# A two-layer decoder with routed experts: phases of the last groups' latents, a block table in three pieces, and later slots for the empty rows

## The chip, the core and the metric

The kernel runs on one core of a Trainium2 chip. A core has engines that work side by side, each taking its own instructions strictly in order: PE multiplies matrices, DVE (vector), ACT (scalar) and POOL (general) work on elements, and SP does little but issue DMA transfers. They wait for each other by semaphores. Matmuls write to PSUM, which holds eight banks of 128 x 512 floats here; the other engines read the banks and so empty them. The metric is device time in microseconds (us) of a whole execution.

## The reference

It is a decoder of two layers over 32 batches of 128 tokens, 128 wide, with a context of 128 tokens by 96 per batch. Each of six blocks is added to x after a normalization. Cut to what matters:

```python
x = x + self_attention(ln(x))          # 16 heads of 8, rotated
x = x + cross_attention(ln(x), ctx)    # 16 heads of 8
x = x + gated_experts(ln(x))           # 8 routed (top 2), 2 shared, width 64
x = x + causal_attention(ln(x))        # 16 heads of 8, rotated
x = x + latents(ctx, ln(x), mask)      # the block that the change moves
x = x + experts(ln(x))                 # 8 experts, top 2, width 512, relu

def latents(ctx, lat, mask):           # 2 heads of 64
    lat, c = layernorm(lat), layernorm(ctx)
    q = lat @ Wq.T
    k, v = split(concat([c @ Wkv.T, lat @ Wlkv.T]))
    q, k = rmsnorm(q) * 64**-0.5, rmsnorm(k)
    return softmax(where(mask, q @ k.T, -max)) @ v @ Wo.T + bo

def experts(x):
    w, i = top_k(softmax(x @ router_w + router_b), 2);  w = w / sum(w)
    y[t, e] = relu(x[t] @ w1[e] + b1[e]) @ w2[e] + b2[e]
    return sum of w * y over the two chosen experts of each token
```

So each token of the latents attends to 256 keys, its batch's 128 latents and 128 context tokens, and each token of the last block goes to two of eight experts.

## The kernel before

**The plan.** The 32 batches are in 8 groups of 4; x stays on chip. The order on every engine is written out by hand. The three attentions of 16 heads give the beat: each is worked off in slots, two per batch, 64 per stage, 192 in all (`attention`). Everything else is laid beside them with `at(slot, phase, function)`. A loop walks through the slots and issues, in each, these phases in this order: "open", "pre", the slot's attention matmuls with their maxima and exps, "inner", the matmuls with the values of an earlier slot, "turn", "turned", "mid", "post". After slot 196 or so no attention is left, and a slot is only what was laid into it. Phases are not barriers: they fix the order in which each engine, SP and POOL's DMA issues among them, gets its instructions.

**Latents** (`latent_attention`). Group g starts at a slot d (L1244: two slots after its causal attention is done): d = 187 for group 5, 195 for group 6, 203 for group 7. In `plan_group`, statistics come at d, the norm's scales on POOL (L1082) at d + 1, the norm on ACT at d + 2 and d + 3, a transpose (L1111), q, k and v of the four batches (L1121) at d + 4 and d + 5, then sums of squares (L997), a pow on POOL (L1139) and the unit heads. Batch i of the group follows with t = d + 8 + 2i in `plan_batch`:

- `fetch` (t - 2, "mid"): SP loads the batch's context keys and values, `lkv<-kv` (L1181); three buffers.
- `turn` (t, "mid"): two transposes of q and k into one bank, emptied by ACT (L1186, L1188, L1189).
- `score` (t + 1, "mid"): per head a mask matmul and a score matmul (L1195, L1200), a maximum on DVE (L1206) and an exp on ACT (L1207).
- `turn_e` (t + 2, "mid"): four transposes of the exps into one bank, copied by DVE into leT (L1216).
- `weigh` (t + 3, "mid"): four matmuls with the values (L1226), then a reciprocal and a product on DVE into lon (L1230, L1232).

`leave` (d + 18, "mid") transposes the group's result, `project` (d + 19, "post") multiplies it by Wo (L1168) and adds it to x. All of these take PSUM banks from one pool, `ps_m`, whose three banks are handed out in turn: `turn`, `turn_e`, `weigh`, `leave`, `project` and each q, k, v take one, `score` takes two, and each waits until the bank of three takings before has been read.

**Router and slots.** From d + 19 on `plan_route` (L1588) chooses two experts per token and scatters the tokens' rows (128 numbers, a target, a gate) with indirect DMAs on POOL (L1729) into the `slots` of the experts in memory. There are three sets of slots, for groups 0 to 3, 4 and 5, and 6 and 7 (parts 0, 1, 2). Rows that no token takes must hold an empty row, whose target lies outside the result; `preset` (L2053) writes them from `nowhere` before any token comes, four transfers per part on SP, 2210 KB each for part 0, 1170 KB for the others. `once` lays preset n into slot 4 + 4n, "mid" (L2075).

**Experts** (`expert_blocks`). `table` (L1826) works out on DVE, on one partition, which expert and which 128 slots belong to each block of the part; the last operation writes the numbers that other engines read into registers. Then, for pairs of blocks: `fetch` on SP (`bx<-slots`, L1868), `weights` on ACT and DVE (a copy out of all experts' weights, L1871), `turn` (L1887, L1889), `hidden` (L1897; relu on ACT L1903 and DVE L1905), `result` (L1914; gates L1921, L1923), `leave` on POOL (an indirect DMA to y, L1928). `plan_part` (L1977) begins the parts at slots 209, 229 and 241, with 20, 12 and 12 pairs, one a slot from two slots later on; the table comes four slots ahead, four fetches are issued at once in the first slot, and each later slot issues one pair more. All experts' weights are loaded on SP in slots 205 on ("open", L1966, L1967).

**Gated experts** of the first layer lie beside the second attention. Each group writes its gates to memory and loads them back spread over the partitions, `g<-spread` (L921), two transfers on SP with a hold of x (L364) issued behind them; POOL and DVE multiply by them (L941), and PE uses the products (L950).

Of the kernel before, what the change touches and what calls it, by code (L numbers as in the profile page):

```python
# [11 lines left out]
F32 = mybir.dt.float32  # L12
# [16 lines left out]
E = 8  # L29
# [84 lines left out]
def decoder(ctx: ExitStack, tc: tile.TileContext, a: dict, out: bass.AP):  # L114
# [132 lines left out]
    def wide(t, shape, axis):  # L247
        return t.unsqueeze(axis).to_broadcast(shape)
# [809 lines left out]
    def latent_attention(lazy, kv, row, bias, masked, plan_route):  # L1058
# [12 lines left out]
        def plan_group(at, g, d):  # L1071
# [98 lines left out]
                nc.vector.tensor_tensor(xf, ps, xf, ALU.add)  # L1170

            at(d + 18, "mid", leave)
            at(d + 19, "post", project)
            plan_route(at, g, d + 19)

        def plan_batch(at, m, g, i, t):
# [57 lines left out]
                )  # L1234

            at(t - 2, "mid", fetch)
            at(t, "mid", turn)
            at(t + 1, "mid", score)
            at(t + 2, "mid", turn_e)
            at(t + 3, "mid", weigh)  # L1240

        def beside(at, done):
            for g in range(G):
# [575 lines left out]
    def expert_blocks(f, total, lazy):  # L1819

        room, nb, top_slot = ROOM[f], NB[f], SLOTS[f] - BLOCK
        y = tc.dram_tile([2 * room, D], F32, name=f"y{f}")
        state = {}
        where = []

        def table():  # L1826

            def row(shape, tag, dtype=F32):
                return lazy["blocks"].tile([1] + shape, dtype, tag="tb_" + tag, name="tb_" + tag, bufs=2 if tag == "where" else 1)

            count, blocks, end, skip = row([E], "count"), row([E], "blocks"), row([E], "end"), row([E], "skip")
            nc.vector.tensor_tensor(count, total[:1], e_base[f][:1], ALU.subtract)
            more = row([E, room // BLOCK], "more")
            nc.vector.tensor_tensor(
                more, wide(count, [1, E, room // BLOCK], 2), wide(starts[:1, : room // BLOCK], [1, E, room // BLOCK], 1), ALU.is_gt
            )
            nc.vector.tensor_reduce(blocks, more, AX.X, ALU.add)
            upto = row([E, E], "upto")
            nc.vector.tensor_tensor(upto, wide(blocks, [1, E, E], 1), until[:1], ALU.mult)
            nc.vector.tensor_reduce(end, upto, AX.X, ALU.add)  # L1840
            nc.vector.tensor_scalar(skip, blocks, -float(BLOCK), float(room), ALU.mult, ALU.add)
            past, t = row([nb, E], "past"), row([nb, E], "past_t")
            first = row([3, nb], "first")
            nc.vector.tensor_tensor(past, wide(end, [1, nb, E], 1), wide(numbers[:1, :nb], [1, nb, E], 2), ALU.is_le)
            nc.vector.tensor_reduce(first[:, 0, :], past, AX.X, ALU.add)
            nc.vector.tensor_tensor(t, past, wide(skip, [1, nb, E], 1), ALU.mult)
            nc.vector.tensor_reduce(first[:, 1, :], t, AX.X, ALU.add)
            nc.vector.tensor_tensor(first[:, 1, :], first[:, 1, :], starts[:1, :nb], ALU.add)
            nc.vector.tensor_scalar(first[:, 2, :], first[:, 0, :], float(E - 1), 512.0, ALU.min, ALU.mult)
            nc.vector.tensor_scalar(first[:, 0, :], first[:, 0, :], float(E - 1), float(W1), ALU.min, ALU.mult)  # L1850
            where.append(row([3, nb], "where", I32))
            nc.vector.tensor_copy(where[0], first)
# [95 lines left out]
            nc.gpsimd.tensor_tensor(one, one, two, ALU.add)  # L1948
            nc.vector.tensor_tensor(X[g], X[g], one, ALU.add)

        return table, fetch, weights, turn, hidden, result, leave, gather, finish

    def experts(halves, lazy, heads, late):

        def beside(at, done):
            def swap():
                heads.close()
                lazy["blocks"] = late.enter_context(tc.tile_pool(name="blocks", bufs=3, reuse_waits="tile"))

            def keep(e):  # L1960
                def fn():
                    rows = a["w_f"][e * P : (e + 1) * P]
                    if e == 0:
                        for tag, n in (("w1", W1), ("w2", 512)):
                            lazy[tag] = lazy["blocks"].tile([P, E * n], F32, tag=tag, name="all_" + tag, bufs=1)
                    nc.sync.dma_start(lazy["w1"][:, e * W1 : (e + 1) * W1], rows[:, :W1])  # L1966
                    nc.sync.dma_start(lazy["w2"][:, e * 512 : (e + 1) * 512], rows[:, W1:])  # L1967
                return fn

            at(done(2, G - 1) + 2, "open", swap)  # L1970
            for e in range(E):
                at(done(2, G - 1) + 2 + e, "open", keep(e))
            begins = [done(2, 3) + 40]
            begins.append(max(begins[0] + (NB[0] + 1) // 2, done(2, 5) + 40))
            begins.append(max(begins[1] + (NB[1] + 1) // 2, done(2, 7) + 33))

            def plan_part(f):  # L1977
                table, fetch, weights, turn, hidden, result, leave, gather, finish = halves[f]
                t = begins[f]
                pairs = (NB[f] + 1) // 2  # L1980
                at(t - 4, "mid", table)
                for i in range(4):
                    at(t, "post", lambda i=i: fetch(i))
                for i in range(2):
                    at(t + i, "post", lambda i=i: weights(i))
                at(t + 1, "post", lambda: turn(0))
                for i in range(pairs):
                    s = t + 2 + i
                    if i + 1 < pairs:
                        at(s, "pre", lambda i=i: turn(i + 1))  # L1990
                    at(s, "inner", lambda i=i: hidden(i))
                    at(s + 1, "post", lambda i=i: result(i))
                    at(s + 2, "mid", lambda i=i: leave(i))
                    if i + 4 < pairs:
                        at(s, "post", lambda i=i: fetch(i + 4))
                    if i + 2 < pairs:
                        at(s, "post", lambda i=i: weights(i + 2))
                if f + 1 < len(PARTS):
                    for n, g in enumerate(PARTS[f]):
                        at(begins[f + 1] + 6 + 2 * n, "post", lambda g=g: gather(g))  # L2000
                        at(begins[f + 1] + 8 + 2 * n, "post", lambda g=g: finish(g))
                        at(begins[f + 1] + 10 + 2 * n, "post", lambda g=g: store(g))

            for f in range(len(PARTS)):
                plan_part(f)
        return beside
# [46 lines left out]
    def preset(n):  # L2053

        chunks = SLOTS[n // 4] // (2 * P)
        part = slots[n // 4].rearrange("(c p r) w -> p c (r w)", p=P, r=2)[:, n % 4 * chunks // 4 : (n % 4 + 1) * chunks // 4]
        nc.sync.dma_start(
            part, nowhere.rearrange("p r w -> p (r w)").unsqueeze(1).to_broadcast([P, chunks // 4, 2 * ROW])
        )

    def once(at, done):
# [10 lines left out]
        at(107, "mid", lambda: folded_bias(w_o1, b_v1, b_o1, bias1))  # L2072
        at(108, "mid", lambda: folded_bias(w_xo1, b_vl, b_xo1, bias_l))
        for n in range(4 * len(PARTS)):
            at(4 + 4 * n, "mid", lambda n=n: preset(n))  # L2075
        guard = []
        at(138, "mid", lambda: guard.append(cross_guard(word)))
        at(140, "mid", lambda: guard[0]())
# [1 line left out]
    lazy, late = {}, ExitStack()  # L2080
# [123 lines left out]
```

## Time and profile before

| what | value |
|---|---|
| device time, median of 3 runs | 1142.7 us (1142.59 to 1147.51) |
| the profiled execution | 1184.79 us, its span 1183.1 us |
| mean granted clock of PE | 0.943 of full speed |
| PE matmul, busy | 1067.5 us (90%) in 12495 instructions |
| DVE, busy | 823.1 us (70%) in 2424 |
| POOL, busy | 645.3 us (55%) in 918 |
| ACT, busy | 615.8 us (52%) in 1440 |
| chain of work that ended last, by engine | PE 52%, DVE 19%, POOL 10%, ACT 7%, issue 6%, DMA 4% |
| moved by DMA | 71.24 MB, of these 37.02 MB written to memory |

The shares are means over stages that differ. Cut at the landmarks of the plan, PE is busy 168.52 of the first 190 us (start and first attention), 635.66 of the 671 up to 861 (second and third attention), 54.91 of the 67 up to 928 (no attention left, no expert matmul yet), 70.25 of the 78 up to 1006 (experts with the last latents beside them), 80.83 of the 99 up to 1105, and 57.33 of the last 78. The granted clock of these stretches is 0.95, 0.98, 0.70, 0.93, 0.88 and 0.90.

How to read the lines shown further on. An instruction in a timeline has its start and its length in us, the engine, the line of the code and the operation, then what it writes and reads; brackets hold the idle time of the engine just before it and what ended it. SPq is SP issuing a DMA: the start is that of the issue, not of the transfer. In the chain of waits each line is one step, start and length first. In a table by stretch the numbers behind an engine are busy us and, in brackets, a count of instructions.

### The profile page before, as it was taken

The page shows a single profiled execution, that of the slowest core. Times are in us where ns is not written, and L with a number is a line of the kernel's source. Part 1 is how long each engine was busy: PE and PEld are TensorE (multiplying, and loading weights), DVE is VectorE, ACT ScalarE, POOL GpSimd, SP SyncE. Part 2 cuts the span into 40 slices and gives each one's busy share as a digit, 9 for nine tenths or more (in the row PEclk, how much of TensorE's full clock was granted, in tenths as well). Part 3 has the DMA queues.
Part 4 walks back from the last instruction along what each step waited for, and adds up shares of the span by engine and source line. Part 5 has one row for each costly group of instructions (what it writes and reads, how often), then busy time and mean ns, then how long its engine had stood idle before and what let it go on. Part 6 is the DMA issues. An engine that isn't in the chain of part 4 may idle for free.

```text
span 1183.1 us, 32419 instructions
## 1 busy us (share of the span) xinstructions
PE 1067.5 (90%) x12495; PEld 829.2 (70%) x12495; DVE 823.1 (70%) x2424; ACT 615.8 (52%) x1440; POOL 645.3 (55%) x918
## 2 busy tenths in 40 slices
PE   6999999999999999999998999989988888788893
PEld 3666667677767776677667677767766778678893
DVE  4678878878778666867787788778666565454652
ACT  2356555676655555554555666744633543333551
POOL 4576656434442544235647675746837245555653
PEclk9999989999999999999999999989976899888997
DMA  8753331000121011110110000001115222123432
GB/s 204 220 154 101 101 100 61 29 29 29 38 47 46 7 41 37 38 26 14 38 46 7 11 15 15 16 11 35 31 37 157 69 56 58 38 66 86 107 109 77
DMA packets 77858, 71.24 MB, mean 60 GB/s; under 512 B 14554, under 2 KB 66829, under 8 KB 77696
## 3 DMA queue, kind: packets, MB, share of 16 engines
q1 hardware_dynamic: 72640, 60.08, 18.7%
q0 software_dynamic: 4768, 8.47, 2.1%
q8 instruction: 102, 1.67, 0.6%
q10 hardware_dynamic: 288, 0.52, 0.1%
q14 instruction: 60, 0.49, 0.1%
HBM read 33.39 MB, written 37.02 MB: 60 GB/s over the span
## 4 chain that ended last, share of the span: by engine, by line
PE 52%; DVE 19%; POOL 10%; ACT 7%; issue 6%; DMA 4%; SPq 0%; another core or an unknown queue 0%; DVEq 0%; POOLq 0%; ACTq 0%
PE bank L633 11%; PE bank L1897 5%; PE bank L661 5%; PE bank L1914 5%; DVE msc L636 5%; PE bank L950 3%; DMA g<-spread 3%; POOL h L941 2%; ACT e L644 2%; PE bank L1121 2%; PE bank L511 1%; PE bank L932 1%; DVE qa L540 1%; PE bank L1200 1%; PE bank L1226 1%
## 5 line engine op out<-in xcount | busy, mean ns | idle before, releaser
L644 ACT ACTIVATE e<-bank 128x512 f32<-128x512 f32 x384 | 207.6, 593 | 178.5 <-PE bank L633 174.2
L636 DVE TENSOR_REDUCE msc<-bank 128x4 f32<-128x512 f32 x384 | 245.2, 680 | 70.1 <-PE bank L633 67.1
L633 PE MATMUL bank<-kb,qz 32*128 32x256 f32 x1536 | 243.8, 410 | 12.3 <-DVE msc L636 10.5
L633 PE MATMUL bank<-qa,kb 32*128 32x128 f32 x3072 | 235.9, 289 | 4.5 <-ACT e L644 4.5
L633 PEld LDWEIGHTS bank<-qa,kb 32*128 32x128 f32 x3072 | 196.6, 191 | 9.7 <-ACT e L644 8.8
L633 PEld LDWEIGHTS bank<-kb,qz 32*128 32x128 f32 x1536 | 146.8, 190 | 65.1 <-DVE msc L636 33.2
L1928 POOL DMA_INDIRECT y<-bo,bx x85 | 85.3, 1004 | 81.5 <-ACT bo L1921 44.0
L647 POOL TENSOR_SCALAR_AFFINE_SELECT e<-e 128x512 f32<-128x512 f32 x128 | 79.2, 642 | 69.5 <-ACT e L644 69.2
L661 PE MATMUL bank<-e,vt 128*32 128x128 f32 x3072 | 109.3, 284 | 0.5 <-POOL e L647 0.5
L1897 PE MATMUL bank<-bxT,w 128*128 128x128 f32 x680 | 92.1, 287 | 9.9 <-issue 9.4
L1897 PEld LDWEIGHTS bank<-bxT,w 128*128 128x128 f32 x680 | 85.9, 202 | 12.5 <-issue 12.0
L1914 PE MATMUL bank<-all_w,bh 128*128 x680 | 91.3, 289 | 3.6 <-issue 3.5
L661 PEld LDWEIGHTS bank<-e,vt 128*32 128x32 f32 x3072 | 81.5, 113 | 15.7 <-POOL e L647 1.5
L1914 PEld LDWEIGHTS bank<-all_w,bh 128*128 128x128 f32 x680 | 85.6, 204 | 6.0 <-issue 5.7
L1729 POOL DMA_INDIRECT slots<-rows,r_ati x64 | 63.6, 994 | 34.0 <-issue 18.4
L1905 DVE TENSOR_SCALAR bh<-bank,w 128x128 f32<-128x128 f32 x164 | 46.1, 343 | 43.8 <-remote 19.6
L941 POOL TENSOR_TENSOR h<-h,g 128x512 f32<-128x512 f32 x30 | 38.7, 1298 | 68.9 <-DMA g<-spread 58.3
L338 ACT ACTIVATE xn<-x,ln_nb,ln_rs 128x128 f32<-128x128 f32 x96 | 42.0, 492 | 49.9 <-POOL ln_nb L332 49.3
L1903 ACT ACTIVATE bh<-bank,w 128x128 f32<-128x128 f32 x176 | 50.3, 368 | 19.9 <-remote 7.7
L1207 ACT ACTIVATE le<-bank,lmx 128x256 f32<-128x256 f32 x64 | 26.9, 471 | 64.7 <-DVE lmx L1206 60.3
L540 DVE SCALAR_TENSOR_TENSOR qa<-bank,head_rows,qz 128x128 f32<-128x128 f32 x192 | 57.6, 342 | 0.0
L1921 ACT ACTIVATE bo<-bank,bx 128x128 f32<-128x128 f32 x44 | 16.2, 368 | 76.2 <-PE bank L1914 47.8
(337 smaller groups left out, 2320.5 us busy)
## 6 DMA issues: line engine op xcount, KB each, us to landing
slots<-nowhere SPq DMA_DIRECT2D x8, 1170.0 KB
slots<-nowhere SPq DMA_DIRECT2D x4, 2210.0 KB
g<-spread SPq DMA_DIRECT2D x16, 512.0 KB
bx<-slots SPq DMA_DIRECT2D x85, 65.0 KB
kv<-kcv SPq DMA_DIRECT2D x8, 516.0 KB
lkv<-kv SPq DMA_DIRECT2D x32, 129.0 KB
yg<-y SPq DMA_DIRECT2D x14, 256.0 KB
all_w<-in_w_f SPq DMA_DIRECT2D x8, 258.0 KB
```

Source lines behind the costliest of these rows:

```text
L540: nc.vector.scalar_tensor_tensor(s["qa"][:, u, :], s["mp"], head_rows[:, 1 - u : 2 - u], m["qz"][:, u, i * P : (i + 1) * P], ALU.mult, ALU.add
L633: nc.tensor.matmul(o, l, r, start=start, stop=stop, skip_group_check=True)
L636: nc.vector.tensor_reduce(tops(MSC[bb % 4], 2 * h + j), sc[j].rearrange("p (s n k) -> p s n k", s=2, n=2), AX.X, ALU.max, negate=True)
L644: nc.scalar.activation(e.rearrange("p n q -> p (n q)"), tr[j], AF.Exp, scale=SCALE)
L647: nc.gpsimd.affine_select(out=e, in_=e, compare_op=ALU.is_ge, fill=0.0, base=0, pattern=[[0, 4], [1, P]], channel_multiplier=-1)
L661: nc.tensor.matmul(s3["av"][32 * n : 32 * n + 32, h3 * P : (h3 + 1) * P], m3["vt"][:, i3, h3, n, u, :], es[u][:, n, :], start=(h3 == 0 and ...
L941: engine.tensor_tensor(m["h"][:, c, :], m["h"][:, c, :], m["g"][:, c, :], ALU.mult)
L1729: ins = nc.gpsimd.indirect_dma_start(slots[f], bass.IndirectOffsetOnAxis(ap=m["ati"][:, c, n : n + 1], axis=0), m["rows"][c][:, n, :], Non ...
L1897: nc.tensor.matmul(ps[:, c * P : (c + 1) * P], w[:, c * P : (c + 1) * P], s["xT"][:, u * P : (u + 1) * P], start=True, stop=True)
L1903: nc.scalar.activation(h, p, AF.Relu, bias=bias)
L1914: nc.tensor.matmul(ps[:, u * P : (u + 1) * P], s["h"][:, u, c, :], lazy["w2"][:, bass.ds(at_w + c * P, P)], start=(c == 0), stop=(c == 3),)
L1928: ins = nc.gpsimd.indirect_dma_start(y, bass.IndirectOffsetOnAxis(ap=x[:, D : D + 1].bitcast(U32), axis=0), s["o"][:, u, :], None, bounds_ ...
```

## The change

Three edits, none of which adds or removes an operation.

1. For groups 5, 6 and 7 the four steps of a batch's latents go to other phases of the same slots: `turn` and `score` from "mid" to "pre", that is ahead of what the slot does for attention or experts, `turn_e` and `weigh` from "mid" to "post", behind all of it. The projection of these groups goes from "post" to "mid". `fetch` and `leave` stay.
2. `table` is cut into three functions with the same 13 DVE operations: `table_counts` (count and number of blocks of each expert), `table_ends` (last block of each expert, expert of each block) and `table_firsts` (first slot of each block, and the numbers in their final form). They are laid at four, three and two slots ahead of the part's begin, "post", instead of one at four ahead, "mid". The rows that are passed on are kept in a dictionary, tb.
3. The presets go from slots 4 + 4n, "mid" (4 to 48) to slots 20 + 8n, "post" (20 to 108).

```diff
@@ -1170,7 +1170,7 @@
                 nc.vector.tensor_tensor(xf, ps, xf, ALU.add)
 
             at(d + 18, "mid", leave)
-            at(d + 19, "post", project)
+            at(d + 19, "mid" if g >= 5 else "post", project)
             plan_route(at, g, d + 19)
 
         def plan_batch(at, m, g, i, t):
@@ -1234,10 +1234,11 @@
                 )
 
             at(t - 2, "mid", fetch)
-            at(t, "mid", turn)
-            at(t + 1, "mid", score)
-            at(t + 2, "mid", turn_e)
-            at(t + 3, "mid", weigh)
+            early, late = ("pre", "post") if g >= 5 else ("mid", "mid")
+            at(t, early, turn)
+            at(t + 1, early, score)
+            at(t + 2, late, turn_e)
+            at(t + 3, late, weigh)
 
         def beside(at, done):
             for g in range(G):
@@ -1823,11 +1824,14 @@
         state = {}
         where = []
 
-        def table():
-
-            def row(shape, tag, dtype=F32):
-                return lazy["blocks"].tile([1] + shape, dtype, tag="tb_" + tag, name="tb_" + tag, bufs=2 if tag == "where" else 1)
-
+
+        tb = {}
+
+        def row(shape, tag, dtype=F32):
+            tb[tag] = lazy["blocks"].tile([1] + shape, dtype, tag="tb_" + tag, name="tb_" + tag, bufs=2 if tag == "where" else 1)
+            return tb[tag]
+
+        def table_counts():
             count, blocks, end, skip = row([E], "count"), row([E], "blocks"), row([E], "end"), row([E], "skip")
             nc.vector.tensor_tensor(count, total[:1], e_base[f][:1], ALU.subtract)
             more = row([E, room // BLOCK], "more")
@@ -1835,14 +1839,18 @@
                 more, wide(count, [1, E, room // BLOCK], 2), wide(starts[:1, : room // BLOCK], [1, E, room // BLOCK], 1), ALU.is_gt
             )
             nc.vector.tensor_reduce(blocks, more, AX.X, ALU.add)
-            upto = row([E, E], "upto")
+
+        def table_ends():
+            blocks, end, skip, upto = tb["blocks"], tb["end"], tb["skip"], row([E, E], "upto")
             nc.vector.tensor_tensor(upto, wide(blocks, [1, E, E], 1), until[:1], ALU.mult)
             nc.vector.tensor_reduce(end, upto, AX.X, ALU.add)
             nc.vector.tensor_scalar(skip, blocks, -float(BLOCK), float(room), ALU.mult, ALU.add)
-            past, t = row([nb, E], "past"), row([nb, E], "past_t")
-            first = row([3, nb], "first")
+            past, first = row([nb, E], "past"), row([3, nb], "first")
             nc.vector.tensor_tensor(past, wide(end, [1, nb, E], 1), wide(numbers[:1, :nb], [1, nb, E], 2), ALU.is_le)
             nc.vector.tensor_reduce(first[:, 0, :], past, AX.X, ALU.add)
+
+        def table_firsts():
+            past, first, skip, t = tb["past"], tb["first"], tb["skip"], row([nb, E], "past_t")
             nc.vector.tensor_tensor(t, past, wide(skip, [1, nb, E], 1), ALU.mult)
             nc.vector.tensor_reduce(first[:, 1, :], t, AX.X, ALU.add)
             nc.vector.tensor_tensor(first[:, 1, :], first[:, 1, :], starts[:1, :nb], ALU.add)
@@ -1948,7 +1956,7 @@
             nc.gpsimd.tensor_tensor(one, one, two, ALU.add)
             nc.vector.tensor_tensor(X[g], X[g], one, ALU.add)
 
-        return table, fetch, weights, turn, hidden, result, leave, gather, finish
+        return (table_counts, table_ends, table_firsts), fetch, weights, turn, hidden, result, leave, gather, finish
 
     def experts(halves, lazy, heads, late):
 
@@ -1975,10 +1983,11 @@
             begins.append(max(begins[1] + (NB[1] + 1) // 2, done(2, 7) + 33))
 
             def plan_part(f):
-                table, fetch, weights, turn, hidden, result, leave, gather, finish = halves[f]
+                tables, fetch, weights, turn, hidden, result, leave, gather, finish = halves[f]
                 t = begins[f]
                 pairs = (NB[f] + 1) // 2
-                at(t - 4, "mid", table)
+                for n, table in enumerate(tables):
+                    at(t - 4 + n, "post", table)
                 for i in range(4):
                     at(t, "post", lambda i=i: fetch(i))
                 for i in range(2):
@@ -2072,7 +2081,7 @@
         at(107, "mid", lambda: folded_bias(w_o1, b_v1, b_o1, bias1))
         at(108, "mid", lambda: folded_bias(w_xo1, b_vl, b_xo1, bias_l))
         for n in range(4 * len(PARTS)):
-            at(4 + 4 * n, "mid", lambda n=n: preset(n))
+            at(20 + 8 * n, "post", lambda n=n: preset(n))
         guard = []
         at(138, "mid", lambda: guard.append(cross_guard(word)))
         at(140, "mid", lambda: guard[0]())
```

## The prediction

> **What bounds the kernel now.** I read the chain of waits first, stretch by stretch, then the busy time by stretch, then the timelines of PE, POOL and SP where the change lands. Slots are turned into times by landmarks: the first expert matmul (L1897) belongs to slot 211 and starts at 928 us, the last attention matmuls of slot 196 at 858 us. Groups 5, 6 and 7 begin their latents at slots 187, 195 and 203, so their batches' turn, score, turn_e and weigh lie in slots 195 to 220, that is 857 to 1000 us. Busy time by stretch (columns: stretch, length, busy us of PE, weight load, DVE, ACT, POOL with counts, granted clock, DMA share, GB/s):
>
> ```profile
> 861.00:893.00 32.00, 27.14 (x173) 19.90 (x172) 20.79 (x71) 10.96 (x29) 11.31 (x19) 0.77 0.13 38
> 893.00:928.00 35.00, 27.77 (x121) 18.68 (x121) 23.05 (x74) 15.92 (x41) 25.10 (x32) 0.65 0.57 167
> 928.00:1006.00 78.00, 70.25 (x562) 66.01 (x561) 46.11 (x172) 33.49 (x95) 34.25 (x42) 0.93 0.20 52
> ```
>
> The reader sees two stretches in which PE is given 0.77 and 0.65 of its clock and still has holes, and a third, the experts with latents beside them, in which PE is 90% busy. In the second one POOL works 25.10 of 35 us, and its timeline shows it without a pause from 887.7 to 915.6 (idle before and its releaser stand in brackets):
>
> ```profile
> 887.72 1.68 POOL L1139 TENSOR_TENSOR nrml<-nrml,half 128x8 f32<-128x8 f32 x1 [6.82 <-DVE nrml L997]
> ...
> 906.24 0.24 POOL L1094 TENSOR_SCALAR ll_nb<-ll_nb 128x4 f32<-128x4 f32 x1
> ...
> 914.65 0.97 POOL L1729 DMA_INDIRECT slots<-rows,r_ati  x1 [0.30 <-issue]
> ```
>
> POOL waits 6.82 us for group 6's first sum of squares, then works off the router's scatters of groups 2 and 3 and group 7's norm scales. SP and PE hang on its end:
>
> ```profile
> 915.33 0.33 SPq L1181 DMA_DIRECT2D lkv<-kv  x1
> 917.25 6.25 SPq L1868 DMA_DIRECT2D bx<-slots  x8
> 923.61 0.37 SPq L1966 DMA_DIRECT2D all_w<-in_w_f  x1
> ```
> ```profile
> 927.54 0.69 PE L1887 MATMUL bank<-ident,bx 128*128 128x128 f32 x2 [1.94 <-DVE bxT L1889]
> 928.03 3.62 PE L1897 MATMUL bank<-bxT,w 128*128 128x128 f32 x16
> ```
>
> Last scatter over at 915.6, blocks fetched from 917.25 (eight issues, 6.25 us), last piece of the weights issued behind them at 923.6, experts from 928.0. So the start of the experts is set by SP, SP by POOL and by the weigh of slot 208 (the fetch at 915.33 waits for it), and POOL by group 6's qkv.
>
> **Part 1: the moves within a slot.** Nothing is added or removed: 12 batches keep their 18 matmul instructions. What changes is the order in every in-order queue. Before, PE runs turn_e(i), turn(i+1) in one "mid" and weigh(i), score(i+1) in the next: turn_e stands just behind the exp it needs (1.08 us of PE hole at 896.17), weigh just behind its copy. Afterwards score opens the slot, other work stands between, and the values close it.
>
> *Slots 196 to 210.* In slot 200 group 6's qkv (L1121) stands behind weigh and score. Today: leT copy on DVE 878.0, then two statistics and lqk at 879.4; weigh 880.6, score 882.5, L1121 from 883.65; sum of squares at 886.95; POOL at 887.72. Afterwards leT (0.69) and weigh (1.1) come behind L1121, and score can start near 879.8. But three PSUM banks in a ring make L1121's bank wait for the exp of the score now ahead of it: score 1.0, maximum 0.42, exp 0.47, so L1121 at about 881.7 instead of 883.65. Two pieces at the full clock take 1.9 instead of 2.93 us. The sum then ends near 883.9 and POOL starts at 884.3: 3.4 us earlier. POOL's own work up to the last scatter is 28 us without holes and does not shrink, so its end moves to about 912.2.
>
> The other gate: the kv fetch of slot 209 waits for the weigh of slot 208, which now stands behind group 7's qkv. Queued behind that fetch on SP are the eight block fetches and the last weights; the expert matmuls wait for these. Worked down from the scales (906.5 - 3.4): apply 1.7, L1111 and copy 1.5, two qkv 1.6, copies 0.8, score 1.1, maximum and exp 1.0, qkv to 911.7, weigh to 912.7, against 915.2 today. After the fetch, today's row leaves 1.9 us to the first block, part of it the wait for the scatters to land; so the first block goes at about 914.1, and the experts move from 928.0 by **-3.1 us**. Ends: 0 (the weigh comes no earlier) and -8 (the 28 us of POOL need not be waited out).
>
> A rule is weighed here. The Trainium skill ("TensorE: Matmul & The Clock Gate", section "HAM oscillation — how this bites in real kernels") says that holes over about 3.4 us cool the clock. In 893 to 928 no PE hole exceeds 1.94 us, and the row says 0.65. By the rule, closing such holes gains nothing on the clock; by the row, a warm PE would do the 54.9 busy us of 861 to 928, at a mean clock of 0.71, in 39, so 16 us less were PE the bound. It isn't, POOL is; I count nothing for the clock beyond L1121, and keep 1.7 us (the first L1897 block, 3.62 against 1.95 later) for the low end.
>
> *Slots 211 to 222.* The chain, word for word:
>
> ```profile
> 949.97 0.23 DVE r_picks L1664
> 950.23 0.22 DVE r_both L1686
> 950.57 0.30 DVE lon L1232
> 951.01 1.13 PE bank L1168 x8
> ```
>
> Group 6's projection needs the bank that weigh filled; DVE empties it (lon) only behind the router's choice: a PE hole of 1.71 us. In "mid", and with weigh at the end, its bank is turn_e's of the slot before, long copied: **-1.7**. The hole of 0.49 before the weigh at 961.6 goes likewise (leT behind the ranks): **-0.5**. Two larger holes, 2.46 before L1186 at 972.0 and 2.36 before L1195 at 983.1, wait for banks that ACT empties late (rgT, rT) for no cause that the trace names. The new order uses other banks; the gain is between 0 and 4.8, and I take 0, because what held ACT will probably hold PE elsewhere. What is now ahead: score's maxima (0.76 on DVE, 0.84 for the exps on ACT) stand before the evictions of the experts. Those need L1897, which starts after the score anyway, about 2.3 us into the slot, when the exps are done: 0, and at most 0.3 a slot where it isn't, 1.5 for five score slots.
>
> **Part 2: the table.** The 13 DVE operations are the same (about 4.2 us for part 0, 3.4 and 4.4 for the others) in three pieces. Part 0 (904.3 to 908.5) delays L1111 by 1.1 us; that is inside the -3.1. Part 1 (1032.4 to 1035.8) shows no PE hole. Part 2:
>
> ```profile
> 1103.44 0.44 PE L1887 MATMUL bank<-ident,bx 128*128 128x128 f32 x2 [1.53 <-DVE bxT L1889]
> ```
>
> A slot there is about 4.3 us and DVE's share 2.3, so a piece of at most 1.7 fits: **-1.5** (ends 0 and -1.5). The table is ready two slots later. Part 1's first fetch goes from 1037.4 to about 1047; eight issues of 0.85 us and a landing end near 1056, before the first turn at 1061. That cover is 5 us; without it each later us costs one.
>
> **Part 3: the empty rows.** 12 transfers on SP, now spread over slots 20 to 108. Today five are issued from 40.7 to 65 us and the rest behind the kv stores. No PE hole up to 200 us is released by a DMA, so taking them away there gains 0. Moved past SP's waits, three of them (slots 92, 100, 108) are now issued right behind the loads g<-spread of three groups, on the same queue. The Trainium skill ("DMA: Bandwidth & Descriptors", section "Two DMAs through the same engine are not ordered") says that descriptors of one queue start in order but are pipelined: by that the load ahead is hardly hurt, 0. Against it: one of 1170 KB takes about 3.5 us by the measured 330 GB/s, and the chain holds the load four times (7.6 us each), so 3 x 3.5 = 10.5 us if the engines were shared evenly and all of it counted. In the trace the store of X that is issued behind such a load today starts its packets only as the load's last ones end, so I take 0 and keep 10.5.
>
> **Sum:** -3.1 - 1.7 - 0.5 - 1.5 = -6.8 us. The profiled execution took 1184.79 us (span 1183.1), 42 us over the median of 1142.7; the stalls that nobody explains may be part of that, and none of them is in my sum. I take the difference as it stands: 1178.0 profiled, **1135.9 us** measured.
>
> **Rivals.**
> - *The gate on SP stays* (0.15): the weigh of slot 208 ends no earlier and the experts start at 928. For it: it now stands behind two more matmuls. Against: its chain begins 3.4 us sooner. 1142.7 - 3.7 = 1139.0.
> - *More comes loose* (0.20): PE warm at the first block (1.7), the two unexplained holes gone (4.8), POOL partly off the path (3 more of the 8): 16.3 less, 1126.4.
> - *The empty rows delay the gates' loads* (0.20): place, slots 88 to 106; PE already waits 13.1 us for POOL's products there (L950). Price up to 3.5 a load; it outweighs the gain from 2.3 a load. 1142.7 + 10.5 - 6.8 = 1146.4, and 1149.5 if the gate on SP also stays. Against it: PE is 8.00 of 8 us busy from 373 to 381 during such a load.
> - The forecast: 0.40. For something not named, slower: 0.05.
>
> **Numbers.** Runs of this kernel spread by 0.4%, so a measurement tells about 0.5% (5.7 us) from no change: faster is below 1137.0, slower above 1148.4. Of the forecast 0.26 falls below 1137.0 and 0.14 above; all of the second rival is faster; of the SP gate 0.02 is; the third splits evenly between same and slower. Faster 0.48, same 0.37, slower 0.15. The range runs from the second rival's time to just past the third's, 1126 to 1147; the forecast's own is 1131 to 1141.
>
> **What would show it.** The pow at L1139 for group 6 some 3 us earlier against the last attention matmuls; POOL still gapless from there to its last scatter; first bx<-slots and first L1897 about 3 us sooner; no hole before L1168 of group 6 and before L1887 at part 2's table; g<-spread still about 7.6 us. It is wrong if the experts start as late as today, if the loads reach 10 us, or if the gain lies before slot 195.

## The result: slower by 0.9 %

The changed kernel took 1155.2 us (median of 17 runs, 1150.0 to 1159.8), the kernel before in the same sessions 1145.5 us (17 runs, 1139.9 to 1149.0): a ratio of 1.0090, 95 % interval 1.0073 to 1.0107. Forecast were 1135.9 us, a gain of 6.8; it is a loss of about 10.

The profiled execution of the changed kernel took 1156.4 us (span 1154.7). It can't be laid beside the first profile of before: that one took 1184.79 us, 36 more than the slowest of the 17 timed runs. So the kernel before was profiled once more, unchanged (run *before_again*, 1150.05 us, span 1148.3), and everything below is compared with this second profile. In the changed kernel's listing the lines from the table on are 8 further down (L1868 is L1876, L1887 is L1895, L1897 is L1905, L1914 is L1922, L1966 is L1974), those of the router one (L1729 is L1730). Of the runs in the table of experiments, one execution of *presets_at_loads*, 1295.8 us, is left out of its ratio.

Busy time by stretch of the changed kernel, the three stretches that the prediction showed:

```profile
861.00:893.00 32.00, 25.80 (x164) 18.26 (x157) 23.11 (x78) 12.16 (x32) 14.74 (x18) 0.87 0.26 77
893.00:928.00 35.00, 23.22 (x96) 16.24 (x96) 18.95 (x54) 13.51 (x35) 19.29 (x27) 0.65 0.44 131
928.00:1006.00 78.00, 76.08 (x632) 72.00 (x632) 53.47 (x198) 37.84 (x107) 40.75 (x48) 0.95 0.21 58
```

and the middle one in the second profile of before:

```profile
893.00:928.00 35.00, 29.07 (x146) 21.82 (x146) 20.89 (x66) 18.51 (x49) 20.12 (x28) 0.70 0.46 131
```

PE gets 23.22 us of work done in this stretch instead of 29.07; the experts begin inside it in one and barely in the other. SP's issues show where it hangs. Changed kernel:

```profile
914.89 0.33 SPq L1181 DMA_DIRECT2D lkv<-kv  x1
916.04 6.25 SPq L1876 DMA_DIRECT2D bx<-slots  x8
922.39 0.37 SPq L1974 DMA_DIRECT2D all_w<-in_w_f  x1
```

Second profile of before:

```profile
907.57 0.33 SPq L1181 DMA_DIRECT2D lkv<-kv  x1
910.36 6.25 SPq L1868 DMA_DIRECT2D bx<-slots  x8
916.71 0.37 SPq L1966 DMA_DIRECT2D all_w<-in_w_f  x1
```

The fetch of slot 209 goes at 914.89 instead of 907.57, and the eight blocks behind it 5.7 us later. What the fetch waits for is on PE, the weigh of slot 208; SP's waits from 895 to 935 in the changed kernel (line, releaser, us in total, times, longest):

```profile
SPq L1181 <- PE bank L1226: 18.5, 2, 9.8
```

PE of the changed kernel:

```profile
899.49 1.61 PE L1111 MATMUL bank<-ident,lat 128*128 128x128 f32 x4 [3.09 <-ACT le L1207]
...
902.92 2.65 PE L1121 MATMUL bank<-w_lat,lT 128*128 128x384 f32 x4
...
907.68 0.54 PE L1195 MATMUL bank<-masked,ident_b 32*128 32x128 bf16 x2 [1.67 <-ACT lv L1123]
...
908.78 1.65 PE L1121 MATMUL bank<-w_lat,lT 128*128 128x384 f32 x2
911.58 1.65 PE L1121 MATMUL bank<-w_lat,lT 128*128 128x384 f32 x2 [1.15 <-ACT le L1207]
...
914.20 0.63 PE L1226 MATMUL bank<-lkv,leT 128*128 128x65 f32 x2
...
926.45 3.27 PE L1905 MATMUL bank<-bxT,w 128*128 128x128 f32 x16
```

Second profile of before:

```profile
901.27 1.09 PE L1111 MATMUL bank<-ident,lat 128*128 128x128 f32 x4 [0.89 <-DVE lon L1232]
...
904.88 1.56 PE L1121 MATMUL bank<-w_lat,lT 128*128 128x384 f32 x4
906.40 0.44 PE L1226 MATMUL bank<-lv,leT 128*128 128x65 f32 x2
...
907.12 0.39 PE L1226 MATMUL bank<-lkv,leT 128*128 128x65 f32 x2
908.34 1.94 PE L1121 MATMUL bank<-w_lat,lT 128*128 128x384 f32 x4
...
920.90 3.62 PE L1897 MATMUL bank<-bxT,w 128*128 128x128 f32 x16
```

From L1111 of group 7, which follows POOL's scales in both, before does two pieces of q, k, v, then the weigh that frees the buffer (over at 907.5, 6.2 us after L1111), then the other two. In the changed kernel all four pieces, the score and its exps stand ahead of that weigh, with two waits for banks (1.67 and 1.15 us): it ends 15.3 us after L1111. The first expert matmul follows L1111 by 26.96 us instead of 19.63.

DVE adds to it. Table of part 0, changed kernel, and POOL's timeline with group 7's scales (L1094) and the instruction beside the table's second piece (L1106):

```profile
903.14 1.82 DVE L1845 TENSOR_TENSOR tb_upto<-tb_blocks,until 1x64 f32<-1x64 f32 x1
...
909.69 0.21 DVE L1860 CAST tb_where<-tb_first 1x117 int32<-1x117 f32 x1
```
```profile
897.92 0.24 POOL L1094 TENSOR_SCALAR ll_nb<-ll_nb 128x4 f32<-128x4 f32 x1
...
903.59 1.28 POOL L1106 TENSOR_TENSOR x<-x,bias_l 128x512 f32<-128x512 f32 x1
...
910.80 0.25 POOL L1619 TENSOR_SCALAR r_rs<-r_mv 128x8 f32<-128x8 f32 x1 [3.49 <-DVE r_mv L1614]
```

and the same table in the second profile of before:

```profile
897.53 0.21 DVE L1839 TENSOR_TENSOR tb_upto<-tb_blocks,until 1x64 f32<-1x64 f32 x1
...
900.51 0.21 DVE L1852 CAST tb_where<-tb_first 1x117 int32<-1x117 f32 x1
```

Before, the whole table was over at 900.7, while PE waited for POOL's scales (ready at 899.8); it cost no more than the 0.89 us that L1111 then waits for lon. Now its second and third piece stand at 903.1 to 909.9, among the router's statistics, the copies of q and k, leT and the maxima, and POOL, which used to go on without a pause, idles 3.49 us for the statistics (r_mv).

### The profile page after: what moved, and what is told of

The parts are those of the page before. It is cut to its first block, busy times and chain, and to the rows that moved or that the text cites. A ratio compares the mean times of both kernels' runs of the same rounds, so it can differ in the third digit from the quotient of the medians.

```text
span 1154.7 us, 32410 instructions
## 1 busy us (share of the span) xinstructions
PE 1048.7 (91%) x12495; PEld 815.1 (71%) x12495; DVE 824.0 (71%) x2424; ACT 615.0 (53%) x1440; POOL 646.9 (56%) x918
## 3 DMA queue, kind: packets, MB, share of 16 engines
q8 instruction: 102, 1.67, 0.6%
## 4 chain that ended last, share of the span: by engine, by line
PE 57%; DVE 18%; POOL 9%; ACT 8%; issue 5%; DMA 2%; SPq 1%; DVEq 0%; POOLq 0%; ACTq 0%
PE bank L633 13%; PE bank L1922 6%; PE bank L661 6%; PE bank L1905 5%; DVE msc L636 5%; PE bank L950 3%; PE bank L932 3%; PE bank L933 2%; ACT e L644 2%; POOL h L941 2%; PE bank L511 2%; PE bank L486 1%; PE bank L1121 1%; POOL slots L1730 1%; DVE qa L540 1%
## 5 line engine op out<-in xcount | busy, mean ns | idle before, releaser
L644 ACT ACTIVATE e<-bank 128x512 f32<-128x512 f32 x384 | 207.6, 593 | 172.0 <-PE bank L633 171.5
L633 PE MATMUL bank<-kb,qz 32*128 32x256 f32 x1536 | 242.0, 408 | 12.3 <-DVE msc L636 10.4
L633 PE MATMUL bank<-qa,kb 32*128 32x128 f32 x3072 | 233.5, 287 | 5.2 <-ACT e L644 5.2
L661 PEld LDWEIGHTS bank<-e,vt 128*32 128x32 f32 x3072 | 80.0, 112 | 15.3 <-POOL e L647 2.0
L1922 PE MATMUL bank<-all_w,bh 128*128 x680 | 88.5, 286 | 0.3 <-issue 0.2
L1905 PE MATMUL bank<-bxT,w 128*128 128x128 f32 x680 | 85.0, 279 | 0.0
L1922 PEld LDWEIGHTS bank<-all_w,bh 128*128 128x128 f32 x680 | 83.9, 201 | 1.2 <-issue 0.9
L1905 PEld LDWEIGHTS bank<-bxT,w 128*128 128x128 f32 x680 | 81.7, 196 | 0.0
L1730 POOL DMA_INDIRECT slots<-rows,r_ati x64 | 63.7, 995 | 30.6 <-issue 16.7
```

Of the source, the lines that this page charges most:

```text
L633: nc.tensor.matmul(o, l, r, start=start, stop=stop, skip_group_check=True)
L644: nc.scalar.activation(e.rearrange("p n q -> p (n q)"), tr[j], AF.Exp, scale=SCALE)
L661: nc.tensor.matmul(s3["av"][32 * n : 32 * n + 32, h3 * P : (h3 + 1) * P], m3["vt"][:, i3, h3, n, u, :], es[u][:, n, :], start=(h3 == 0 and ...
L1730: ins = nc.gpsimd.indirect_dma_start(slots[f], bass.IndirectOffsetOnAxis(ap=m["ati"][:, c, n : n + 1], axis=0), m["rows"][c][:, n, :], Non ...
L1905: nc.tensor.matmul(ps[:, c * P : (c + 1) * P], w[:, c * P : (c + 1) * P], s["xT"][:, u * P : (u + 1) * P], start=True, stop=True)
L1922: nc.tensor.matmul(ps[:, u * P : (u + 1) * P], s["h"][:, u, c, :], lazy["w2"][:, bass.ds(at_w + c * P, P)], start=(c == 0), stop=(c == 3),)
```

## Experiments

Up to the 377th exp of the attention the kernels differ in nothing but the place of the empty rows, and still the profiles take 838 to 850 us for it, at mean granted clocks of 0.99 to 0.97. So I compare stretches that begin at a landmark. *Blocks* and *start* are the time from the first L1111 of group 7 to the first issue of bx<-slots and to the first expert matmul; *part 1* is from the 73rd to the 81st relu on ACT (L1903, four per pair; group 7's router and the change to part 1 lie there), *part 2* from there to the 121st (the table of part 2). All from the timelines of the profiles, in us; the ratio is that of the timed runs to before. The stretch from the first expert matmul to the 73rd relu is left out: it takes 103.1 to 106.1 us with the old order of the latents beside the experts and 101.3 to 105.4 with the new one, and most of this spread goes with the granted clock.

| run | blocks | start | part 1 | part 2 | ratio, 95 % interval |
|---|---|---|---|---|---|
| before_again | 9.08 | 19.63 | 10.51 | 39.91 | 1.0007 (0.9989 to 1.0025) |
| changed kernel | 16.55 | 26.96 | 13.44 | 38.31 | 1.0090 (1.0073 to 1.0107) |
| presets_back | 16.55 | 27.40 | 13.12 | 38.31 | 1.0049 (1.0020 to 1.0078) |
| table_at_once | 11.63 | 22.44 | 10.52 | 39.89 | 1.0046 (1.0031 to 1.0060) |
| latents_back | 11.02 | 24.87 | 13.02 | 38.31 | 1.0058 (1.0037 to 1.0079) |
| presets_alone | 9.90 | 20.55 | 10.52 | 39.89 | 1.0031 (1.0012 to 1.0050) |
| latents_alone | 11.89 | 22.55 | 10.45 | 39.89 | 1.0037 (1.0017 to 1.0057) |
| table_alone | 11.95 | 25.55 | 13.01 | 38.31 | 1.0053 (1.0034 to 1.0071) |
| after_4buf | 11.19 | 24.18 | 13.05 | 38.31 | 1.0044 (1.0025 to 1.0064) |
| table_earlier | 9.99 | 20.51 | 10.57 | 38.32 | 0.9988 (0.9964 to 1.0013) |
| presets_by_68 | 8.25 | 19.03 | 10.53 | 39.93 | 0.9998 (0.9975 to 1.0020) |
| presets_at_loads | 9.45 | 20.03 | 10.52 | 39.88 | 1.0012 (0.9987 to 1.0036) |
| picked | 8.20 | 18.97 | 10.51 | 38.32 | 0.9988 (0.9969 to 1.0007) |
| latents_4buf | 9.27 | 20.52 | 10.84 | 39.60 | 0.9962 (0.9945 to 0.9980) |
| mended | 9.25 | 20.49 | 10.87 | 38.26 | 0.9957 (0.9940 to 0.9975) |
| presets_again | 9.93 | 20.74 | 10.47 | 39.89 | 0.9998 (0.9979 to 1.0018) |

**The kernel before, again.** No edit.

> The kernel before, unchanged, for a second profile: the first one took 1184.79 us against runs of 1140 to 1149, with pieces of idle time on PE between 980 and 1080 us that no instruction explains. If those were of that one execution, this profile takes about 1145 us, has no such stalls, and the ratio is 1.000 within 0.003. If they belong to the kernel under the profiler, it takes about 1185 us again.

1150.05 us when profiled, ratio 1.0007. The scattered idle time of the first profile was of that execution alone, the holes of 2.46 and 2.36 us at 972 and 983 included: none of them is there.

**One part undone at a time.**

```diff
 presets_back
-            at(20 + 8 * n, "post", lambda n=n: preset(n))
+            at(4 + 4 * n, "mid", lambda n=n: preset(n))
 table_at_once
-                    at(t - 4 + n, "post", table)
+                    at(t - 4, "mid", table)
 latents_back
-            early, late = ("pre", "post") if g >= 5 else ("mid", "mid")
+            early, late = "mid", "mid"
-            at(d + 19, "mid" if g >= 5 else "post", project)
+            at(d + 19, "post", project)
```

> The changed kernel with the empty rows written in slots 4 to 48 as before; latents and table as changed. If the later writing of the empty rows delays the gates' loads (the rival of the prediction that ends slower, 10.5 us), this takes about 1145 us, ratio to before 1.000. If the cost lies in the latents or the table, it stays at about 1155 us, ratio 1.009.

> The changed kernel with the three pieces of the table one after the other at four slots ahead, mid, as the whole table stood before; latents and empty rows as changed. If the table that is ready two slots later delays the first fetches of parts 1 and 2 (the cover of 5 us that the prediction counted is gone), this takes about 1147 us, ratio 1.002. If not, about 1155 us, ratio 1.009.

> The changed kernel with the phases of groups 5 to 7 as before (turn, score, turn_e and weigh in mid, the projection in post); table and empty rows as changed. If the moves within the slots make the latents of these groups slower (the weigh of a batch, and with it the fetch behind it, end later; score's maxima and exps stand ahead of the experts' evictions), this takes about 1145 us, ratio 1.000. If the forecast for this part was right (a gain of 5.3 us), it takes about 1160 us, ratio 1.013.

Each of the three takes away a third to a half of the loss, none all of it: I had expected one culprit. *presets_back* rests on 8 runs of 1147 to 1159 us, its interval touches the changed kernel's, and its columns are those of the changed kernel; so what came back there is not shown to be the empty rows'. The columns tell the other two parts apart. Where the table is in late pieces, part 1 takes 2.5 to 2.9 us longer and part 2 is 1.6 shorter; the start is late with either of the two parts, and latest with both. In latents_back SP's last piece of the weights (slot 210; they are loaded from slot 203 on, not 205) waits for DVE, which comes late to its copy of the first weights behind the table. SP's waits from 895 to 935, columns line, releaser, us in total, times, longest:

```profile
SPq L1974 <- DVE w L1887: 2.3, 1, 2.3
```

That is why there the start lies 13.9 us behind the blocks instead of 10.5.

**One part alone.** The kernel before with one of the three edits as the change has it.

> The kernel before with nothing changed but the empty rows, slots 20 to 108. If their later writing costs by itself, as presets_back hinted (0.4 % came back when it was undone), this takes 4 to 5 us more than before, ratio 1.004. If the loads of the gates do not mind them, ratio 1.000 to 1.002.

> The kernel before with only the phases of groups 5 to 7 changed. Theory now: the weigh of slot 208 stands behind the matmuls of group 7's q, k, v, SP's fetch behind it, the blocks behind the fetch: the experts start about 2.7 us later against POOL's scales (from the profile of table_at_once), and 2 to 3 us come back while experts and latents run together: ratio 1.000, within 0.002. If the moves in themselves are the loss, ratio 1.004 or more; the forecast for this part was 0.995.

> The kernel before with only the table in three pieces. Theory now: pieces two and three fall into DVE's busy stretch at slots 206 and 207, ahead of the router's statistics, the copy of leT and the maxima, where the whole table stood in DVE's idle time; the experts start 5 us later against POOL's scales (profile of latents_back), part 1 loses 2.5 more at the router's choice, part 2 gains 1.7: 5 to 6 us, ratio 1.005. If the table costs only through the later fetches, ratio 1.000 to 1.002.

The table alone costs 0.53 %, as expected from its columns: start 5.9 us later than in before_again, part 1 2.5 longer, part 2 1.6 shorter, and L1111 itself up to 0.9 earlier, since no table stands before it (this last term is argued; the scatter ahead of L1111 hides it): 5.9 together against 6.1 measured. The latents alone cost 0.37 %, where I had expected none: 2.9 us at the start, and less came back later than I thought. The two make 0.90 %, the whole change, with 0.2 % of uncertainty on each. For the empty rows 0.31 % came out, but no column and no other stretch of the profile shows it.

**A fourth buffer.** In the changed kernel:

```diff
-                s["kv"] = opened().tile([P, KV], F32, tag="kv", name="lkv", bufs=3)
+                s["kv"] = opened().tile([P, KV], F32, tag="kv", name="lkv", bufs=4)
```

> The changed kernel with four buffers for lkv instead of three, so that the fetch of slot 209 waits for the weigh of slot 206 and no longer for that of slot 208. If this fetch is what holds the blocks on SP, bx<-slots goes at about 910 us instead of 916, the experts start up to 5 us earlier, and the time falls to about 1150 us, ratio 1.005. If the pieces of the table on DVE hold the start as well, bx goes earlier and the experts do not: 1154 to 1156 us, ratio 1.008.

Half of the loss is gone (1.0044). The blocks go 11.19 us behind L1111 instead of 16.55, not at once: SP now waits for the table, whose last operation ends 10.4 us behind L1111. So three gates stand one behind the other on SP: the scatters (over 6.6 to 8.6 us behind L1111 in all profiles), the table, the fetch. The start itself moves by 2.8 us only, since DVE's backlog delays the copies of weights as in latents_back.

**The table earlier, the empty rows elsewhere, a selection.**

```diff
 table_earlier (table_alone with)
-                    at(t - 4 + n, "post", table)
+                    at(t - 6 + n, "post", table)
 presets_by_68
-            at(4 + 4 * n, "mid", lambda n=n: preset(n))
+            at(20 + 4 * n, "post", lambda n=n: preset(n))
 presets_at_loads
-            at(4 + 4 * n, "mid", lambda n=n: preset(n))
+            at(92 + 8 * (n % 3), "post", lambda n=n: preset(n))
 picked (against before)
+            phase = lambda s, p: p if s > 210 else "mid"
...
-            at(t + 3, "mid", weigh)
+            at(t + 3, phase(t + 3, "post"), weigh)
...
-            at(d + 19, "post", project)
+            at(d + 19, "mid" if g >= 6 else "post", project)
...
+                    at(t - 4 + n if f == 2 else t - 4, "post" if f == 2 else "mid", table)
```

> The kernel before with the table in the same three pieces, but six, five and four slots ahead of a part's begin instead of four, three and two (slots 203 to 205 for part 0). If it is the place on DVE that costs, and not the cutting: the experts start as early as before (77.6 us after the landmark of the last attention exps instead of 83.6), the 2.6 us of part 1 are gone, the 1.6 us of part 2 stay: ratio 0.9985 to 1.000. If the cutting itself costs, it stays at 1.005.

> The kernel before with the empty rows in slots 20 to 64 (20 + 4n, post), so that none is issued near a group's loads of the gates. If the 0.3 % of presets_alone come from the last three, behind these loads, ratio 1.000; if they come from leaving the start (slots 4 to 20), 1.003.

> The kernel before with all twelve transfers of empty rows behind the gates' loads of three groups (slots 92, 100 and 108, four each). If such a transfer slows the load ahead of it, as the prediction's rival has it, the cost is four times that of presets_alone: POOL waits 20 us or more longer for g<-spread, ratio 1.01. If not, ratio 1.003 or less and POOL's waits as before.

> The kernel before with what the profiles show to gain and without what they show to lose: the phases of the latents moved only in slots from 211 on (behind the experts' start), the projection only for groups 6 and 7, the table in pieces only for part 2, the empty rows as before. The experts start as before; 1.6 us come from part 2, 1 to 3 us from the latents beside the experts: ratio 0.997. If the holes only move elsewhere: 1.000.

The table in pieces costs nothing two slots earlier: the start and part 1 are back, part 2 keeps its gain, 0.9988 against 1.0053. It is the place on DVE, not the cutting. With all twelve transfers of empty rows behind the loads of three groups, SP reads for the second of them, and the chain of waits for the second and third (presets_at_loads):

```profile
368.04 1.24 SPq L921 DMA_DIRECT2D g<-spread  x2
369.32 14.75 SPq L2057 DMA_DIRECT2D slots<-nowhere  x4
```
```profile
368.66 7.83 DMA g<-spread
406.83 7.27 DMA g<-spread
```

Both loads have four transfers behind them and take 7.83 and 7.27 us, as they do without (7.0 to 8.4), POOL waits 26.5 us for all such loads (34.6 in before_again, 19.7 to 58.3 in the other profiles), and the ratio is 1.0012. The load is not slowed by what is issued behind it; what is long is SP's issue of four such transfers, 14.4 to 17.8 us, and there was room for it. *picked* lies between no change and a gain of 0.3 %, which this measurement doesn't separate.

**What was still open.** latents_alone with the fourth buffer; the changed kernel with the table at t - 6, the fourth buffer and the empty rows as before; presets_alone a second time.

> latents_alone with four buffers for lkv: the phases moved, the table and the empty rows as before, and the fetch of slot 209 no longer behind the weigh of slot 208. If that fetch is what the moves cost, ratio 1.000 (latents_alone had 1.0037). If the order on PE and DVE itself costs, it stays at 1.003 to 1.004.

> The changed kernel with what the runs speak against taken out: the table's pieces at six to four slots ahead (1.0053 became 0.9988 there), four buffers for lkv, the empty rows as before. If the two gates on SP were all that the change lost, what is left of it is gain: 1.6 us of part 2 and about 2 us of the latents beside the experts, ratio 0.997. If the moved phases cost in another way too, 1.000 to 1.003.

> presets_alone a second time. No profile shows a place where it loses, and all twelve transfers behind the loads cost 1.0012 at most uncertainly. If its 1.0031 was real, 1.003 again; if it was the scatter of the runs, 1.000 to 1.001.

The fourth buffer turns 1.0037 into 0.9962, more than I had expected (1.000). SP in latents_4buf, whose L1111 is at 902.43:

```profile
905.71 0.33 SPq L1181 DMA_DIRECT2D lkv<-kv  x1
911.70 6.25 SPq L1876 DMA_DIRECT2D bx<-slots  x8
```

The fetch no longer waits for slot 208, and the blocks go 1.4 us after the last scatter, as before. So what the moved phases lost went by that fetch, and with a fourth buffer the kernel gains 0.38 %. No run has the fourth buffer with the old order, so how much of this is the buffer's own stays open. Of the 0.75 % between the two (8.6 us; 5.5 to 11.7 by both intervals) the profiles show 2.0 at the start and 3.1 from there to the 81st relu (101.4 us + 10.8 against 104.9 + 10.4). These 3.1 lie where the granted clock differs: the first to the 9th relu takes 11.1 us at 0.98 against 13.3 at 0.81, the 33rd to the 73rd 50.7 at 0.97 against 51.9 at 0.93; and *presets_back* took 101.3 us up to the 73rd with three buffers. The rest I did not find. *mended* is the fastest, 1142.7 us against 1147.9 of before in the same session, faster by 0.25 to 0.6 %, and not to be told from *latents_4buf*. And the empty rows' 0.31 % did not come again (0.9998): no cost of them is shown.

## Why the prediction was wrong

**The start of the experts, -3.1 us: this step failed, with +7.3 measured.** With part 1 (+2.9) and part 2 (-1.6) that is 8.6 of the loss of about 10. Two terms of the step were mis-sized.

- *POOL's chain 3.4 us earlier.* It did not come. Measured from the start of the 377th exp of the attention (L644, the eighth from the last), the last scatter of part 0 ends after 63.9 us in the changed kernel and 63.6 in before_again; over all profiles 62.0 to 67.3 with the old order (mean 65.1 of 10), 63.9 to 65.7 with the new one (mean 64.8 of 7). The pow of group 6 on POOL starts 36.1 us behind that exp instead of 36.3, and the second two pieces of q, k, v before it take 2.67 us at a granted clock of 0.57, not the 1.9 I had put down. I had seen that weigh and score go from ahead of q, k, v, and not that turn_e of the slot before, which now stands behind the two earlier pieces of q, k, v, waits for their bank, nor that group 6's scales come 1.8 us later. Nor was POOL quite without a pause in the first profile: its second pow waited 0.87 us there. Changed kernel:

```profile
872.44 0.66 PE L1214 MATMUL bank<-ident,le 128*128 128x128 f32 x4 [2.06 <-ACT lv L1123]
```

- *The weigh of slot 208 at 912.7.* Worked down from POOL's scales I had 9.6 us to its end; it took 16.7 (898.2 to 914.8). The order was right, the durations were not: I took 1.6 us for two pieces of q, k, v and no wait for a bank between the second two, where the trace has 2.65 at a granted clock of 0.55, 1.67 and 1.15 of waiting, and the table's two pieces on DVE among the copies that free these banks. The rival "the gate on SP stays" named the right gate, but I gave it a price of 0 where the new order allows for any; it should have been the case to work out first, since a buffer ring of three and an in-order SP stood in the code.

**The table's second sum, also wrong.** I had counted part 0 inside the -3.1 and part 1 as free, because part 1's whole table showed no hole. Late pieces cost 5.9 us at the start and 2.5 at part 1, where the two pieces now lie in front of the router's choice for group 7 on DVE. Changed kernel, then second profile of before:

```profile
1034.36 0.18 PE L1702 MATMUL bank<-r_both,above_b 128*128 128x32 bf16 x1 [2.06 <-DVE r_both L1687]
...
1034.88 3.66 PE L1922 MATMUL bank<-all_w,bh 128*128 x16 [0.25 <-issue]
```
```profile
1028.47 0.18 PE L1701 MATMUL bank<-r_both,above_b 128*128 128x32 bf16 x1 [0.75 <-DVE r_both L1686]
...
1028.99 2.11 PE L1914 MATMUL bank<-all_w,bh 128*128 x16 [0.25 <-issue]
```

The longer wait is 1.3 us of it. The rest is PE's clock: behind the wait the granted clock was 0.50 from 1035.1 to 1038.4, and the same 16 matmuls took 3.66 us instead of 2.11. In all five runs with the table late the wait is 1.62 to 2.06 us and the granted clock of this stretch 0.87; in the other eleven of the table the wait is 0.75 to 0.84 us and the clock 1.00. I had counted nothing for the clock beyond L1121.

I had asked whether a piece fits into DVE's free share of a slot. It does, but not in any place of the slot: what counts is who stands behind it in DVE's queue. table_earlier shows it. The step for part 2 was right: 1.5 forecast, 1.6 measured (39.91 to 38.31), and the later fetches cost nothing, as forecast.

**The latents beside the experts: one hole right, one wrong.** The hole before L1168 (1.70 in before_again) is gone. The one before the weigh, 0.5 in the sum, grew; PE of the changed kernel:

```profile
946.02 1.06 PE L1168 MATMUL bank<-w_xo,loT 128*128 128x128 f32 x8
...
959.86 0.64 PE L1226 MATMUL bank<-lv,leT 128*128 128x65 f32 x2 [1.62 <-ACT le L1207]
```

The weigh now waits for a bank that the score of the same slot fills and the exps empty: again the ring of three banks, in an order I had worked out for slot 200 only. Where the granted clock is 1.00 in both, the 9th to the 33rd relu takes 37.7 us in the new order (presets_back) and 39.0 in the old one (presets_alone), so 1.3 of the forecast 2.2 came; in the changed kernel's own profile the clock was 0.79 from the 17th to the 25th, and it took 40.9. The two unexplained holes, which I had left at 0, were indeed no part of the kernel.

**The empty rows: the load is not delayed, as forecast.** Forecast 0, with 10.5 us for the rival. The load takes as long with one transfer behind it or four; the same kernel gave 1.0031 and 0.9998, 1.0015 on average or 1.7 us. That excludes the rival's 10.5 us, though not a cost of 2 or 3, for which no profile shows a place.

**The base.** I took the difference against the first profile as it stood, saying that 42 us of it were unexplained. None of them was in the sum, but the rival "more comes loose", with a chance of 0.20, took 4.8 of its us from two of these holes.

## What to carry to other kernels

When a step is moved within an in-order plan, follow the buffer that it frees, not only the result that it makes: here three buffers let a weigh moved by half a slot hold a fetch, the fetch held eight others behind it on the same queue, and one more buffer turned a loss of 0.37 % into a gain of 0.38 %. Small work on a side engine that idles for nearly half of each slot is free only where that engine's queue has nobody waiting behind it; ask what stands behind the instruction, and put it where the engine waits for something else. Where a change has several parts, undo and apply each alone: the time of the whole would have hidden an order that gains behind a missing buffer and a late table. And where PE has holes, look at its granted clock before a longer stretch is put down to the wait alone.

## What the hardware showed that was not expected

A DVE operation on one partition, tb_upto, took 0.21 us in all three tables of before_again, and for part 0 1.48 to 1.99 us in the five runs with the late table (1.82 in the changed kernel), where POOL's addition L1106 of 1.3 us ran beside it; in all five it ended 0.08 to 0.09 us after POOL's did. The Trainium skill ("SBUF — State Buffer", section "SBUF: two separate sides") has this: a vector operation with two inputs in SBUF and a GpSimd operation that reads SBUF exclude each other for a whole instruction. The traces agree that one waits for the other's end, and they show the wait inside the recorded time of the DVE operation. The page lets the one that starts first go ahead; the DVE operation starts 0.11 to 0.61 us ahead of POOL's by the record, and it was the one that waited. So a piece of 0.2 us can cost 1.8 where it is placed beside POOL's work.

PE's granted clock fell to 0.50 between 890 and 900 us in before_again, where its longest hole from 880 on was 1.1 us, far below the 3.4 us of the rule that the prediction weighs: no hole of that length was needed here. The time from the 377th exp to L1111 of group 7 lies anywhere between 53.8 us (granted clock 0.89) and 60.7 us (0.72) in the profiles with the old order; the stretches above leave that scatter out.
